# A graph layer's loop with slot 5's sums moved among the products with x, and an end with the left-over sums between the second layers

## The chip, the cores and the metric

One core of a Trainium2 chip runs the kernel. The metric is the device time of one execution in microseconds (us); below it stands as the median of three timed runs. The profile is of one more execution, whose own time is given beside its span.

## The reference

The kernel computes one layer of a graph network over 12,500 nodes and 412,500 edges, which come sorted by their target node `dst`. All numbers are float32, and all edges read the same graph's globals.

```python
h = jnp.maximum(_layernorm(x, axis=-1), 0.0)                    # x: 12500 x 128
agg = jax.ops.segment_sum(edges, dst, num_segments=12500)       # edges: 412500 x 48
u = graph_globals[0]                                            # the same 64 numbers for every node
hid = jax.nn.relu(jnp.concatenate([h, agg, u], axis=1) @ W1 + b1)   # 256 wide
out = x + hid @ W2 + b2                                         # 12500 x 128
```

## The kernel before

**Tiles.** A chunk is 768 edges, 128 partitions of 6; a group is 4 chunks. One iteration of the loop takes 11 groups (33,792 edges) and 1,024 nodes; there are 12 iterations. The very first group is summed ahead of the loop (`prologue`); the last 3,924 edges (5 chunks and 84 more) and 212 nodes are done in the end (`epilogue`). The 11 groups lie in six slots, each with its own buffer: slots 0 to 3 and slot 5 hold two groups, slot 4 one. The nodes of an iteration are block A and block B of 512; the 212 left over are block Z.

**The sum over edges, in two steps.** `sums(s)` multiplies, for each chunk and each of its six edges a partition, a one-hot matrix of 28 columns with 128 x 48 edge numbers (line 681); four chunks lie beside each other in the columns of the array. This gives partial sums in PSUM bank `S[s % 2]`, which ScalarE copies to `ss[s]` (line 685). `place(s)` multiplies these by a one-hot window `pl[s]` of 186 columns (line 703) and so adds them into the banks `agg[0]` (`ax`, block A) and `agg[1]` (`ay`, block B). VectorE makes both kinds of one-hot matrix, `onehots(s)` (line 662) and `places(s)` (line 668); both look one iteration ahead, except that slot 5's last groups reach over into the next iteration's nodes: `place(5, .., 1)` puts their part for this iteration at its end, `place(5, (0,), 0)` the other part at the start of the next.

**The layers.** `stats`, `variance`, `shift` (VectorE, with a square root on ScalarE) and `norm` (ScalarE, line 731) make the normalized x; `turn` transposes it on TensorE (line 740) and copies it back (line 741); `sums_out` copies the aggregates from PSUM (`ags`, line 746). `layers(layer_x)` is four products of W1 with x (line 750), into the banks PH0, PH1, PT, PO; `layers(layer_e)` adds W1 times the aggregates (line 755); `layers(relu)` is ScalarE's bias and relu (line 760). `second` is the product with W2 (line 776), and it runs one iteration later: near the start of an iteration for the nodes of the one before. Its result is added to x + b2 (`add_b`, GpSimd, line 735) and held in SBUF (`hold`, line 780). All held blocks are stored in the end, by `store_held`.

**What sets the order.** The order in which `body` calls these functions is the order of instructions on every engine: each engine takes its own part of the list in turn and waits at the first instruction whose semaphores are not there. `Flow` works out these waits from the names that each operation reads and writes. Loads of edges go out on SP in the order of `add_slots`; a slot's next load waits until its sums are done. Loads of x go out on ScalarE's queue. TensorE's loop is cut at `f.mark = "su4"`, the sums of slot 4: its instructions from there on are the first part of the code that it jumps back to.

In `body`, TensorE's order is sums 0, 1, 2; place 5 (first part), 0, 1; second layers A, B; sums 3, 4, 5; turns A, B; place 2, 3, 4, 5 (second part); products with x; products with the aggregates. In `epilogue` it is the left-over sums (`sur`, line 938), place 5, the turn of Z, the left-over places (`pcr`, line 948), both layers' first products of Z, second layer A, a transpose for the verdict on the indices (`verdict_2`), second layer B, second layer Z.

Of the kernel before, what the change touches and what calls it, by code (L numbers as in the profile page):

```python
# [18 lines left out]
P = 128  # L19
# [7 lines left out]
IN = 1024  # L27
# [25 lines left out]
class Flow:  # L53
# [14 lines left out]
    def op(self, eng, name, reads, writes, emit, dma=False):  # L68
        self.seq.append(dict(eng=eng, name=name, r=tuple(reads), w=tuple(writes), emit=emit, dma=dma, it=self.at))
# [336 lines left out]
def kernel(  # L406
# [40 lines left out]
    S = [bank("s0"), bank("s1")]  # L447
    agg = [bank("ax"), bank("ay")]
    pt = bank("pt")
    ph = [bank("ph0"), bank("ph1")]  # L450
# [60 lines left out]
    A, B, Z = 0, 1, 2  # L511
# [113 lines left out]
    def verdict_1():  # L625
        farthest()
        f.chain("DVE", "wc", ["worst", "farm"], ["wcol"],
            lambda: nc.vector.tensor_scalar(wcol, farm, -(V - 1) / 2, None, OP.add),
            lambda: nc.vector.tensor_tensor(wcol, wcol, worst[:, 2:3], OP.max))
# [40 lines left out]
    def onehots(s):  # L670
        g = SLOTS[s]
        onehot(s, oh[s], ["rel_i"], rel_i[:, g[0] - 1:g[0]] if len(g) == 1 else rel_i[:, g[0] - 1:g[1]:g[1] - g[0]])

    def places(s):
        windows(s, pl[s], ["off_i"], [off_i[:, v - 1:v] for v in SLOTS[s]])
# [15 lines left out]
    def place(s, fresh=(), part=None):  # L691

        groups, sv, pv = SLOTS[s], ss[s], pl[s]
        todo = [(n, j) + v for j, g in enumerate(groups) for n, v in enumerate(pieces(g)) if part is None or v[0] == part]
        todo.sort(key=lambda v: v[2] if len(groups) == 1 else (v[0] if v[1] == 0 else 1 - v[0], v[1]))
        seen = set()

        def emit(i):
            seen.clear()
            out = []  # L700
            for _, j, bk, at, frm, w in todo:
                h = HI * bk
                out.append(nc.tensor.matmul(agg[bk][h:h + DE, at:at + w], sv[:, j], pv[:, j, frm:frm + w],  # L703
                                            start=bk in fresh and bk not in seen, stop=True, skip_group_check=True))
                seen.add(bk)
            return out
        op("PE", f"pc{s}" + ("" if part is None else f".{part}"), [f"ss{s}", f"pl{s}"], [f"bk{b}" for b in sorted({v[2] for v in todo})], emit)
# [21 lines left out]
    def norm(k, m=P):  # L729
        op("ACT", f"xn{k}", [f"x{k}", f"x{k}t", f"sc{k}", f"sh{k}"], [f"xn{k}"], lambda i: [  # L730
            nc.scalar.activation(xn[k][:m, r], xt[k][:m, r], AF.Relu, bias=sh[k][:m, r:r + 1], scale=sc[k][:m, r:r + 1]) for r in range(RR[k])])  # L731
# [5 lines left out]
    def turn(k, m=P, bk=None, key="PT", eng="ACT"):  # L737
        pv = (pt if bk is None else bk)[:, :RR[k] * P].rearrange("p (r c) -> p r c", r=RR[k])
        copy = nc.scalar.copy if eng == "ACT" else nc.vector.tensor_copy
        op("PE", f"tu{k}", [f"xn{k}", "ident"], [key], lambda i: [nc.tensor.transpose(pv[:, r, :m], xn[k][:m, r], ident[:m, :m]) for r in range(RR[k])])  # L740
        op(eng, f"hT{k}", [key], [f"hT{k}"], lambda i: [copy(hT[k][:, :, :m], pv[:, :, :m])])

    def sums_out(k, m=P):
        h, r = HI * (k % 2), RR[k]
        op("ACT", f"ag{k}", [f"bk{k % 2}"], [f"ag{k}"], lambda i: [
            nc.scalar.copy(ag[k // 2][h:h + DE, :, :m], agg[k % 2][h:h + DE, :m * r].rearrange("p (c r) -> p r c", r=r))])
# [17 lines left out]

    middle = [(a, k) + v for a, bs in enumerate(((("PH0", ph[0]), ("PH1", ph[1])), (("PT", pt), ("PO", po)))) for k, v in enumerate(bs)]

    def layers(fn):

        for a, k, key, bk in middle:
            fn(f"{k}.{a}", key, bk.rearrange("p (r c) -> p r c", r=R), k, a)  # L770

    def second(k, m=P, bk=None, key="PO", keep=None):
# [15 lines left out]
    def prologue():  # L788
# [51 lines left out]
        for b in range(NB):  # L840
# [13 lines left out]
        windows(5, pl[5], ["off0"], [off[:, 0:1], off[:, 0:1]])  # L854
        op("PE", "bi", ["w1u", "u"], ["PH1"], lambda i: [
            nc.tensor.matmul(ph[1][:, NG + a:NG + a + 1], w1u[:, a * P:(a + 1) * P], u, start=True, stop=True, skip_group_check=True) for a in range(NH)])
        onehots(2)
        op("DVE", "bj", ["PH1", "b1"], ["bias"], lambda i: [nc.vector.tensor_tensor(bias, ph[1][:, NG:NG + NH], b1_sb, OP.add)])
        dst_3(ph[1], "PH1", range(1, NB))
        fetch_off(1)  # L860
        places(0)
        places(1)
        op("DVE", "spare", [], ["spare"] + [f"di{b}" for b in range(NB)] + [f"di{NB - 1}r", f"di{NB - 1}s"] + [f"df{k}" for k in range(DF)],
           lambda i: [nc.vector.memset(hold[0][:, 0:1], 0.0)])
        for s in (3, 4, 5):
            onehots(s)
        for s in (2, 3, 4):
            places(s)
        op("DVE", "f0", ["rel0.0", "rel0.3"], ["farm"], lambda i: [nc.vector.tensor_reduce(farm, rel[:, :q], AX.X, OP.max, apply_absolute_value=True)])

    def body(it):
        f.at = it

        def add_slots(*some):
            for s in some:
                sums(s)
                if it < NIT - 1:
                    load_e(s, 1)

        keep = lambda i: (i + NIT - 2) % (NIT - 1)  # L880
        farthest()
        fetch(1)
        add_slots(0, 1)
        for k in (A, B):
            stats(k)
            variance(k)
        add_slots(2)
        onehots(0)
        shift(A)
        shift(B)  # L890
        onehots(1)
        onehots(2)
        norm(A)
        norm(B)
        place(5, (0,), 0)
        place(0, (1,))
        place(1)
        places(5)
        fetch_off(1)
        places(0)  # L900
        places(1)
        for k in (A, B):
            second(k, P, ph[k], f"PH{k}", keep)
        for k in (A, B):
            add_b(k)

        add_slots(3, 4, 5)
        for s in (3, 4, 5):
            onehots(s)
        turn(A)  # L910
        turn(B, P, po, "PO")
        if it < NIT - 1:
            load_x(A, lambda i: (i + 1) % NIT * IN)
            load_x(B, lambda i: (i + 1) % NIT * IN + BN)
        for s in (2, 3, 4):
            place(s)
        place(5, (), 1)
        sums_out(A)
        sums_out(B)
        for s in (2, 3, 4):  # L920
            places(s)
        layers(layer_x)
        layers(layer_e)
        layers(relu)

    def epilogue():
        f.at = NIT
        m = RN // RZ
        load_rest()
        store_held()  # L930
        add_b(Z, m)
        stats(Z, m)
        variance(Z, m)
        shift(Z, m)
        norm(Z, m)
        rest = lambda j, c: P if j * CG + c < FULL else TP
        op("PE", "sur", ["oh0", "oh1", "e0.0", "e0.1", "ezt"], ["S0"], lambda i: [
            nc.tensor.matmul(S[0][NV * c:NV * c + V, j * DE:(j + 1) * DE], oh[j][:rest(j, c), c * T + t], e[0][:rest(j, c), j * CG + c, t * DE:(t + 1) * DE],  # L938
                             start=(t == 0), stop=(t == T - 1), skip_group_check=True)
            for j in range(2) for t in range(T) for c in range(min(CG, RC - j * CG))])  # L940
        op("ACT", "ssr", ["S0"], ["ssr"], lambda i: [nc.scalar.copy(ssr.rearrange("p j d -> p (j d)"), S[0][:, :2 * DE])])
        place(5, (0,), 0)
        turn(Z, m, S[1], "S1")
        verdict_0()
        verdict_1()
        todo = [(j,) + v for j, g in enumerate((1, 2)) for v in pieces(g)]
        op("PE", "pcr", ["ssr", "pl0", "pl1"], ["bk0"], lambda i: [
            nc.tensor.matmul(agg[bk][:DE, at:at + w], ssr[:, j], pl[j][:, 0, frm:frm + w], start=False, stop=True, skip_group_check=True)
            for j, bk, at, frm, w in todo])
        sums_out(Z, m)  # L950
        zr = [S[0][:, a * RN:(a + 1) * RN].rearrange("p (r c) -> p r c", r=RZ) for a in range(NH)]
        for a in range(NH):
            layer_x(f"z{a}", "S0", zr[a], Z, a, a == 0, m)
        for a in range(NH):
            layer_e(f"z{a}", "S0", zr[a], Z, a, m)
        for a in range(NH):
            relu(f"z{a}", "S0", zr[a], Z, a, m)
        second(A, P, ph[A], "PH0")
        store(A, lambda i: (i - 1) * IN)
        verdict_2()  # L960
        second(B, P, ph[B], "PH1")
        store(B, lambda i: (i - 1) * IN + BN, eng="ACT")
        second(Z, m, pt, "PT")
        store(Z, lambda i: i * IN, m)
        for e_ in f.of:
            op(e_, f"rb{e_}", ["bad"], [], lambda i, e_=e_: [f.of[e_].reg_load(flag_of[f.of[e_].engine], bad[0:1, 0:1])])
# [48 lines left out]
```

## Time and profile before

| | |
|---|---|
| timed runs | 277.99, 278.39, 282.0 us; median 278.39 |
| profiled execution | 277.39 us, its span 275.6 us |
| TensorE busy | 252.7 us, 92% of the span |
| VectorE busy | 239.5 us, 87% |
| ScalarE, GpSimd busy | 128.2 us, 47%; 54.5 us, 20% |
| DMA | 94.33 MB, 342 GB/s over the span |

The span runs from the first to the last instruction; the profiled execution's time is 1.8 us longer. Rows of a timeline give the start, the length, the engine, the line of the kernel, the operation, the tiles as out<-in, the shape, the number of instructions merged into the row, and in brackets the engine's idle time before it with what ended it. A table by stretches gives for each stretch its length, then busy time and instructions of TensorE's products, its weight loads, VectorE, ScalarE and GpSimd, then the granted TensorE clock, the DMA engines' busy share and GB/s. The lengths of TensorE's rows overlap, since products are pipelined; the distance from start to start is what a step takes.

### The profile page before, as it was taken

The numbers are of one execution on the slowest core, as the hardware profiler recorded it, in microseconds if no ns is written. First come the engines' busy times: TensorE is split into PE (matmuls) and PEld (weight loads), VectorE is DVE, ScalarE is ACT, GpSimd is POOL, SyncE is SP. The second block draws the span as 40 slices with busy tenths as digits, with TensorE's granted clock in tenths as the row PEclk, the third lists the DMA queues.
The fourth block names the chain that finished last, engine by engine and source line by source line (L and its number), as shares of the span: only waits on it lengthen the run. The fifth ranks groups of instructions, "written<-read, shape, count | busy, mean of one in ns | idle before, by whom it ended". The sixth has DMA issues, their size and how long they took to land.

```text
span 275.6 us, 17205 instructions
## 1 busy us (share of the span) xinstructions
PE 252.7 (92%) x7567; PEld 195.6 (71%) x7568; DVE 239.5 (87%) x591; ACT 128.2 (47%) x316; POOL 54.5 (20%) x47
## 2 busy tenths in 40 slices
PE   2946999999999999999999999999999999999990
PEld 2946866867858849859768768578498497597580
DVE  4899997998989989989989979989899899799521
ACT  7800544535437337245445355373373463454520
POOL 8100050040220400500500502304105005007000
PEclk9955999999999999999999999999999999999999
DMA  6999999999999999999999999999999999995992
GB/s 213 297 363 356 341 357 362 356 357 361 356 361 357 356 362 356 356 362 356 356 362 356 356 362 356 359 359 356 362 357 356 362 356 356 362 356 208 368 363 73
DMA packets 79012, 94.33 MB, mean 342 GB/s; under 512 B 3227, under 2 KB 72189, under 8 KB 78998
## 3 DMA queue, kind: packets, MB, share of 16 engines
q1 hardware_dynamic: 75398, 87.63, 96.1%
q10 hardware_dynamic: 3312, 6.03, 6.2%
q0 software_dynamic: 288, 0.49, 0.7%
q8 instruction: 7, 0.11, 0.2%
q14 instruction: 7, 0.06, 0.1%
HBM read 87.75 MB, written 6.40 MB: 342 GB/s over the span
## 4 chain that ended last, share of the span: by engine, by line
PE 87%; SPq 5%; DMA 3%; issue 2%; DVE 0%
PE s L681 27%; PE ph L776 18%; PE ph L750 8%; PE ax L703 7%; SPq L516 5%; PE ph L755 5%; PE po L750 4%; PE pt L750 4%; PE pt L755 4%; DMA e<-in_edge_attr_dram 3%; PE ay L703 3%; PE pt L740 3%; PE po L740 2%; PE s L938 1%; PE s L750 0%
## 5 line engine op out<-in xcount | busy, mean ns | idle before, releaser
L662 DVE TENSOR_TENSOR oh<-iota_v,rel_i 128x1344 f32<-128x1344 f32 (+1 forms) x78 | 130.8, 1716 | 0.0
L681 PEld LDWEIGHTS s<-e,oh 128*28 128x28 f32 x6336 | 75.1, 109 | 23.3 <-issue 21.4
L681 PE MATMUL s<-e,oh 128*28 128x48 f32 x6336 | 80.9, 210 | 11.0 <-issue 6.7
L735 POOL TENSOR_TENSOR xba<-xa,b_sb 128x512 f32<-128x512 f32 x12 | 15.4, 1285 | 198.3 <-DVE holda L780 198.3
L685 ACT COPY ss<-s 128x96 f32<-128x96 f32 (+1 forms) x72 | 16.8, 234 | 70.6 <-PE s L681 70.6
L668 DVE TENSOR_SCALAR pl<-iota_w,off_i 128x186 f32<-128x186 f32 x141 | 35.1, 309 | 0.5
L735 POOL TENSOR_TENSOR xbb<-xb,b_sb 128x512 f32<-128x512 f32 x12 | 31.1, 2591 | 0.0
L760 ACT ACTIVATE hida<-ph,bias 128x512 f32<-128x512 f32 x12 | 8.2, 687 | 42.2 <-PE ph L755 42.2
L703 PE MATMUL ax<-pl,ss 128*48 128x186 f32 (+3 forms) x172 | 27.1, 300 | 0.0
L776 PEld LDWEIGHTS ph<-w,hida 128*128 128x128 f32 x208 | 24.2, 191 | 3.8 <-issue 3.8
L776 PE MATMUL ph<-w,hida 128*128 128x128 f32 x208 | 26.7, 281 | 0.0
L703 PE MATMUL ay<-pl,ss 128*48 128x186 f32 (+3 forms) x168 | 26.3, 297 | 0.0
L776 PE MATMUL ph<-w,hidb 128*128 128x128 f32 x208 | 25.6, 276 | 0.6 <-issue 0.6
L776 PEld LDWEIGHTS ph<-w,hidb 128*128 128x128 f32 x208 | 24.3, 192 | 0.8 <-issue 0.7
L731 ACT ACTIVATE xna<-xa,sha,sca 128x128 f32<-128x128 f32 x48 | 19.8, 482 | 5.1 <-DVE sha L727 5.1
L710 DVE BATCH_NORM_STATS2 sta<-xa 128x6 f32<-128x128 f32 x48 | 10.5, 281 | 12.1 <-DMA xa<-in_x_dram 12.1
L703 PEld LDWEIGHTS ax<-pl,ss 128*48 128x48 f32 x172 | 17.6, 126 | 4.3 <-issue 2.0
L731 ACT ACTIVATE xnb<-xb,shb,scb 128x128 f32<-128x128 f32 x48 | 19.6, 479 | 0.0
L703 PEld LDWEIGHTS ay<-pl,ss 128*48 128x48 f32 x168 | 17.8, 124 | 0.0
L755 PE MATMUL ph<-ags,w1a 48*128 48x512 f32 x48 | 13.5, 641 | 0.0
L750 PE MATMUL ph<-hta,w1h 128*128 128x512 f32 x24 | 13.5, 644 | 0.0
L750 PE MATMUL ph<-htb,w1h 128*128 128x512 f32 x24 | 12.3, 592 | 0.0
(150 smaller groups left out, 301.5 us busy)
## 6 DMA issues: line engine op xcount, KB each, us to landing
e<-in_edge_attr_dram SPq DMA_DIRECT2D x133, 576.0 KB, 10.0
xa<-in_x_dram ACTq DMA_DIRECT2D x11, 256.0 KB, 5.8
xb<-in_x_dram ACTq DMA_DIRECT2D x11, 256.0 KB, 6.3
out_dram<-holda SPq DMA_DIRECT2D x11, 256.0 KB, 3.2
out_dram<-holdb SPq DMA_DIRECT2D x11, 256.0 KB, 3.3
holda<-in_dst_dram SPq DMA_DIRECT2D x4, 384.0 KB, 4.9
e<-in_edge_attr_dram SPq DMA_DIRECT2D x1, 720.0 KB, 8.9
xa<-in_x_dram SPq DMA_DIRECT2D x1, 256.0 KB, 10.5
```

Of the source, the lines that this page charges most:

```text
L516: return [f.of[eng].dma_start(dst_ap(i) if callable(dst_ap) else dst_ap, src_ap(i) if callable(src_ap) else src_ap)]
L662: op("DVE", f"oh{name}", reads + ["iota_v"], [f"oh{name}"], lambda i: [nc.vector.tensor_tensor(ov, iota_v[:, None, None, :].to_broadcast([ ...
L668: nc.vector.tensor_scalar(out[:, j], iota_w, o[j], None, OP.is_equal) for j in range(len(o))])
L681: nc.tensor.matmul(S[k][NV * c:NV * c + V, j * DE:(j + 1) * DE], o[:, (j * CG + c) * T + t], ev[:, j * CG + c, t * DE:(t + 1) * DE], start ...
L685: op("ACT", f"ss{name}", [f"S{k}"], [f"ss{name}"], lambda i: [nc.scalar.copy(sv.rearrange("p j d -> p (j d)"), S[k][:, :m * DE])])
L703: out.append(nc.tensor.matmul(agg[bk][h:h + DE, at:at + w], sv[:, j], pv[:, j, frm:frm + w], start=bk in fresh and bk not in seen, stop=Tr ...
L731: nc.scalar.activation(xn[k][:m, r], xt[k][:m, r], AF.Relu, bias=sh[k][:m, r:r + 1], scale=sc[k][:m, r:r + 1]) for r in range(RR[k])])
L735: nc.gpsimd.tensor_tensor(xb[k][:m], xt[k][:m], b2_sb[:m, None, :].to_broadcast([m, RR[k], D]), OP.add)])
L740: op("PE", f"tu{k}", [f"xn{k}", "ident"], [key], lambda i: [nc.tensor.transpose(pv[:, r, :m], xn[k][:m, r], ident[:m, :m]) for r in range( ...
L750: nc.tensor.matmul(o, w1h[:, a * P:(a + 1) * P], hT[k][:, :, :m], start=first, stop=False, skip_group_check=True)])
L755: nc.tensor.matmul(o, w1a[h:h + DE, a * P:(a + 1) * P], ag[k // 2][h:h + DE, :, :m], start=False, stop=True, skip_group_check=True)])
L776: nc.tensor.matmul(ov[:m, r], hid[k][:, a, r, :m], w2[:, a], start=(a == 0), stop=(a == NH - 1)) for r in range(RR[k]) for a in range(NH)])
```

## The change

In the loop, slot 2's sums move from slot 1's side to behind the second layers; slot 1's place moves from slot 0's side to those of slots 2 to 4; slot 5's sums move behind the turns and these places, and the second part of slot 5's place moves in front of the last of the four products with x. The one-hot matrices follow: those of slot 2 go with slots 3 and 4, those of slot 5 and the windows of slot 1 go later. ScalarE copies block A's aggregates before slot 5's sums instead of after them. In the end, place 5 and the turn of Z come first, then second layer A, then the left-over sums, then second layer B, then the rest of Z's work. In the prologue the order of VectorE's one-hots follows the loop's.

TensorE's order in `body` after: sums 0, 1; place 5 (first part), 0; second layers A, B; sums 2, 3, 4; turns A, B; place 1, 2, 3, 4; sums 5; three products with x; place 5 (second part); the fourth product with x; products with the aggregates. No operation is added or left out.

```diff
-    def layers(fn):
+    def layers(fn, some=middle):
-        for a, k, key, bk in middle:
+        for a, k, key, bk in some:
...
     prologue:
-        onehots(2)
         op("DVE", "bj", ...)
         dst_3(ph[1], "PH1", range(1, NB))
         fetch_off(1)
         places(0)
-        places(1)
+        onehots(2)
         op("DVE", "spare", ...)
-        for s in (3, 4, 5):
+        for s in (3, 4):
             onehots(s)
-        for s in (2, 3, 4):
+        for s in (1, 2, 3, 4):
             places(s)
+        onehots(5)
...
     body:
-        add_slots(2)
         onehots(0)
         shift(A)
         shift(B)
         onehots(1)
-        onehots(2)
         norm(A)
         norm(B)
         place(5, (0,), 0)
         place(0, (1,))
-        place(1)
         places(5)
         fetch_off(1)
         places(0)
-        places(1)
         for k in (A, B):
             second(k, P, ph[k], f"PH{k}", keep)
         for k in (A, B):
             add_b(k)
 
-        add_slots(3, 4, 5)
-        for s in (3, 4, 5):
+        add_slots(2, 3, 4)
+        for s in (2, 3, 4):
             onehots(s)
         turn(A)
         turn(B, P, po, "PO")
         if it < NIT - 1:
             load_x(A, lambda i: (i + 1) % NIT * IN)
             load_x(B, lambda i: (i + 1) % NIT * IN + BN)
-        for s in (2, 3, 4):
+        for s in (1, 2, 3, 4):
             place(s)
+        sums_out(A)
+        for s in (1, 2, 3, 4):
+            places(s)
+        add_slots(5)
+        onehots(5)
+        layers(layer_x, middle[:3])
         place(5, (), 1)
-        sums_out(A)
         sums_out(B)
-        for s in (2, 3, 4):
-            places(s)
-        layers(layer_x)
+        layers(layer_x, middle[3:])
         layers(layer_e)
         layers(relu)
...
     epilogue:
         norm(Z, m)
+        place(5, (0,), 0)
+        turn(Z, m, S[1], "S1")
+        second(A, P, ph[A], "PH0")
+        store(A, lambda i: (i - 1) * IN)
...
         op("PE", "sur", ...)
         op("ACT", "ssr", ...)
-        place(5, (0,), 0)
-        turn(Z, m, S[1], "S1")
         verdict_0()
         verdict_1()
+        second(B, P, ph[B], "PH1")
...
         for a in range(NH):
             relu(f"z{a}", "S0", zr[a], Z, a, m)
-        second(A, P, ph[A], "PH0")
-        store(A, lambda i: (i - 1) * IN)
         verdict_2()
-        second(B, P, ph[B], "PH1")
         store(B, lambda i: (i - 1) * IN + BN, eng="ACT")
         second(Z, m, pt, "PT")
         store(Z, lambda i: i * IN, m)
```

## The prediction, made before the change was run

> **What bounds the kernel now.** I read the page, then the table by stretches of time (two iterations of the loop), the DMA issues, the waits, and last TensorE's timeline of one iteration and of the end.
>
> ```profile
> span 275.6 us, 17205 instructions
> PE 87%; SPq 5%; DMA 3%; issue 2%; DVE 0%
> ```
> ```profile
> 44.71:64.12 19.41, 19.00 (x617) 14.55 (x621) 18.04 (x45) 9.50 (x25) 3.84 (x2) 1.00 1.09 358
> 219.33:238.91 19.58, 19.09 (x619) 14.56 (x621) 18.00 (x44) 9.50 (x25) 3.84 (x2) 1.00 1.09 358
> ```
> ```profile
> e<-in_edge_attr_dram SPq DMA_DIRECT2D x133, 576.0 KB, 10.0
> xa<-in_x_dram ACTq DMA_DIRECT2D x11, 256.0 KB, 5.8
> xb<-in_x_dram ACTq DMA_DIRECT2D x11, 256.0 KB, 6.3
> ```
> ```profile
> PE s L681 <- DMA e<-in_edge_attr_dram: 4.2, 3, 2.5
> ```
>
> The chain that ended last is 87% TensorE. In a stretch of 19.41 us it is busy 19.00; VectorE 18.04, ScalarE 9.50; so a microsecond added to TensorE's stream lengthens an iteration. DMA is a close second bound: an iteration loads 11 x 576 KB of edges and 2 x 256 KB of x, 7.01 MB, which at the 358 GB/s of both rows takes 19.59 us. The early iteration, 19.41, is TensorE's own pace; the late one, 19.58, is the DMA's: edges loaded ahead have been used up. The waits agree: only three waits for edges are listed, 4.2 us, and none of them in the iteration shown next.
>
> One iteration on TensorE (start, length, what):
>
> ```profile
> 141.64 3.50 PE L681 MATMUL s<-e,oh 128*28 128x48 f32 x288
> 145.07 0.48 PE L703 MATMUL ax<-pl,ss 128*48 128x140 f32 x3
> 146.16 2.05 PE L776 MATMUL ph<-w,hida 128*128 128x128 f32 x16
> 148.04 1.95 PE L776 MATMUL ph<-w,hidb 128*128 128x128 f32 x16
> 149.92 1.22 PE L681 MATMUL s<-e,oh 128*28 128x48 f32 x96
> 151.55 1.74 PE L681 MATMUL s<-e,oh 128*28 128x48 f32 x144 [0.41 <-issue]
> 153.22 0.66 PE L740 MATMUL pt<-ident,xna 128*128 128x128 f32 x4
> 154.24 0.36 PE L703 MATMUL ax<-pl,ss 128*48 128x186 f32 x1
> 155.49 1.12 PE L750 MATMUL ph<-hta,w1h 128*128 128x512 f32 x2
> 156.45 1.02 PE L750 MATMUL ph<-htb,w1h 128*128 128x512 f32 x2
> 157.31 1.02 PE L750 MATMUL pt<-hta,w1h 128*128 128x512 f32 x2
> 158.17 1.02 PE L750 MATMUL po<-htb,w1h 128*128 128x512 f32 x2
> 159.12 1.13 PE L755 MATMUL ph<-ags,w1a 48*128 48x512 f32 x4
> ```
>
> From start to start: sums of slots 0 to 2 3.43, places 1.09, second layers 3.76, sums 3 with the loop's jump 1.63, sums 4 and 5 1.67, turns 1.02, places 1.25, products with x 3.63. In the last, a pair in mid-stretch takes 0.86 (156.45 to 157.31), but the first 0.96 and the last 0.95: entering a stretch costs 0.10, leaving it 0.09. The other stretches show the same. At 0.86/1024 = 0.84 ns a column the first places (3 times 2 x 186 columns, two banks at once where they can) are 0.94, and take 1.09; a second layer (16 x 128 columns) is 1.72, and the second one takes 1.88. **So each stretch of one kind costs about 0.15 us beyond its columns.**
>
> **The loop, part by part.** No matrix product is added or removed; the order changes. TensorE's stretches before: sums 0-2, places, second layers, sums 3, jump, sums 4-5, turns, places, x products, aggregate products. After: sums 0-1, places, second layers, sums 2-3, jump, sum 4, turns, places, *sum 5*, three x products, *places 5.1*, the *fourth x product*, aggregate products. Three stretches more, 3 x 0.15 = 0.45. Inside the sums one boundary between slots goes (1|2 and 4|5 are no longer neighbours, 2|3 become so); no row prices it alone: it saves between 0 and a whole stretch's 0.15, and as a slot takes 1.14 in slots 0-2 and 1.11 by 1.67/1.5 in 4-5, starts included, boundaries cannot be cheap; I take 0.15. Net +0.30: 19.70 us an iteration. Bounds: 0, if the new switches overlap, to +0.57, three at 0.19 without the saving.
>
> The Trainium skill speaks against the change here: TensorEngine Tiling, Key Properties, has it that a change of tiling mode drains TensorE. It gives no time; TensorE: Matmul & The Clock Gate, Single matmul latency, puts the part of a warm matmul outside its columns at 166 ns, and three of these, less 0.15, would be an estimate of +0.35, 0.6 us more over the loop than mine.
>
> A row of ScalarE's timeline, a relu over 128 x 512 out of PSUM (the last of the loop), bounds a copy of 48 x 512 from above:
>
> ```profile
> 259.34 0.70 ACT L760 ACTIVATE hidb<-po,bias 128x512 f32<-128x512 f32 x1
> ```
>
> The waits that move cost nothing as far as I see. Sum 2 stands at 3.43 x 2/3 + 0.78 (two of three places) + 3.76 = 6.9 us of the iteration instead of 2.3, sum 5 at 12.6 instead of 10.3: edges have 2 to 4 us more to land, and the DMA no longer sets the late iterations. SP issues loads in the same order, each behind its sum; a load waits 10.0 us from issue to landing, mostly in the queue, so an issue 1 or 2 us later leaves the queue full. VectorE's one-hots and places are used 9 us or more after they are written, most in the next iteration; without that cover each microsecond of them (18.04 busy) would be on the path. On ScalarE, places 5.1 need the copy of sum 5 and the aggregate products need the copy of places 5.1; three x products (2.6) cover the first, the fourth (0.86 + 0.19) the second, at most 0.70 for the copy plus a handover: 0.3 us to spare, and if not, that much an iteration. The x loads leave ScalarE earlier, since the adds of b2 follow second layers that come 1.5 us earlier; VectorE's wait for x shrinks, which no one waits for.
>
> The loop ends where the left-over sums start:
>
> ```profile
> 258.38 2.94 PE L938 MATMUL s<-e,oh 128*28 128x48 f32 x72
> ```
>
> From its second iteration (44.71) to there are 213.67 now, eleven at 19.70 = 216.7 after. **+3.0.**
>
> The first iteration, on arriving edges:
>
> ```profile
> 24.95 2.14 PE L681 MATMUL s<-e,oh 128*28 128x48 f32 x96 [0.40 <-DMA e<-in_edge_attr_dram]
> 33.50 1.22 PE L681 MATMUL s<-e,oh 128*28 128x48 f32 x96
> ```
>
> Sum 2 waits 0.40 for edges and takes 2.14 there, at about half the speed of a sum behind the second layers (33.50, 1.22). After, it stands behind them, with its edges there. Saved 2.1 + 0.4; paid: 1.1 for the sum there, 0.30 for the stretches, and some 0.3 because more of the layers runs at half speed. **-0.8**, between 0 and -1.5.
>
> **The end.** TensorE's rows behind the left-over sums, then ScalarE's and SP's:
>
> ```profile
> 261.25 0.53 PE L703 MATMUL ax<-pl,ss 128*48 128x140 f32 x4
> 261.70 0.40 PE L740 MATMUL s<-ident,xnr 106*128 106x106 f32 x2
> 262.03 0.83 PE L948 MATMUL ax<-pl,ssr 128*48 128x186 f32 x4
> 262.79 0.98 PE L750 MATMUL s<-htr,w1h 128*128 128x212 f32 x4
> 263.71 0.98 PE L755 MATMUL s<-agr,w1a 48*128 48x212 f32 x4
> 264.62 2.05 PE L776 MATMUL ph<-w,hida 128*128 128x128 f32 x16
> 266.62 1.95 PE L776 MATMUL ph<-w,hidb 128*128 128x128 f32 x16
> 268.40 1.04 PE L776 MATMUL pt<-w,hidr 128*106 128x128 f32 x8
> ```
> ```profile
> 260.65 0.88 ACT L731 ACTIVATE xnr<-xr,shr,scr 106x128 f32<-106x128 f32 x2 [0.43 <-DVE shr L727]
> 264.73 0.77 ACT L760 ACTIVATE hidr<-s,bias 128x212 f32<-128x212 f32 x2 [1.50 <-PE s L755]
> ```
> ```profile
> 269.93 0.77 SPq L516 DMA_DIRECT2D out_dram<-otr  x2
> ```
>
> Now TensorE never stands here: the left-over sums (2.87 to the next start) cover ScalarE, which must finish the loop's last relu (at 260.04) and then scale block Z's x until 261.53; both second layers cover the relu of Z (until 265.50). From the loop's end to the last store's issue are 269.93 - 258.38 = 11.55 us.
>
> After, the turn of Z stands second, in front of everything that covered its wait, and TensorE takes its queue in order: second layer A, sums, second layer B and all else stand behind it. From the loop's end: places 0.53, then nothing until x of Z is scaled at 3.15 (261.53 - 258.38), **2.6 us idle**; turn from 3.2 to 3.55; second layer A to 5.45 (1.89: 2.00 from 264.62 to 266.62, less a 0.11 transpose); sums to 8.3; second layer B to 10.2 (1.78 and a switch); places of the rest 0.76 and a switch to 11.1; x products to 12.0; aggregate products from 12.0, and the relu of Z ends 1.79 after their start (263.71 to 265.50), at 13.8, with nothing left to run but the verdict's transpose: **0.9 idle**; the last second layer from 13.85; the store issues 1.53 after that (268.40 to 269.93) and a switch: 15.45. **+3.9.** The adds and stores of A and B come earlier and end earlier; they are not last. The store of A stays behind the held ones on SP, and the store of B goes out on ScalarE behind the relu of Z at 13.9, before the last.
>
> **Sum:** 3.0 - 0.8 + 3.9 = 6.1. The profiled execution took 277.39, so 283.5; the three timed runs (277.99, 278.39, 282.0) stood 0.6 and more above it, so as a timed run **284.1 us**, 2.0% over the median. A measurement of this kernel tells about 2% from no change, so this sits on the line.
>
> **Rivals.**
> *The clock falls in the end's idle stretch.*
>
> ```profile
> 11.65:15.06 3.41, 2.76 (x63) 2.42 (x62) 3.38 (x4) 2.06 (x5) 0.00 (x0) 1.00 1.06 341
> 15.06:18.47 3.41, 1.57 (x80) 1.60 (x84) 3.34 (x12) 0.00 (x0) 0.00 (x0) 0.50 1.09 360
> 267.64:271.06 3.42, 1.80 (x17) 1.59 (x15) 1.24 (x3) 0.00 (x0) 0.00 (x0) 1.00 0.52 192
> 271.06:274.47 3.41, 0.00 (x0) 0.00 (x0) 0.00 (x0) 0.00 (x0) 0.00 (x0) 1.00 0.14 38
> ```
>
> The third number from the end is the granted clock. It fell at 15.06, after a stretch with 0.65 us idle, and did not at 271.06, after one with 1.6 idle. 2.6 idle may be enough; then 3.4 us run at half speed, +1.7: 285.8. The Trainium skill (TensorE: Matmul & The Clock Gate, The HAM clock gate) asks for at least one idle window of about 3.4 us; by that rule this does not happen. The row at 15.06 does not look like that rule, so I leave it 0.2.
>
> *Not slower: the switches in the loop hide under weight loads, and only the waits count.* The place is the loop; it decides if an added stretch costs under 0.03 us. Eleven iterations at TensorE's 19.40 are 213.4 and no longer stretched to the DMA's 19.58 at the end, as edges now have 2 us more: -0.3 - 0.8 + 3.9 = 2.8, 281.0 by the same steps, +0.9%. For it: weight loads do run under products. Against: the 0.96 and 0.95 beside 0.86. 0.25.
>
> *The loads starve.* SP stands in front of load 2 until sum 2 is done at 8.05 of the iteration; if that empties the queue for 0.3 us an iteration, +3.3: 287.4. Against: 10.0 us in the queue. 0.05.
>
> *The end does not stall,* ScalarE having been freed earlier: then 284.1 - 2.6 = 281.5. The order of ScalarE's queue is not changed there: 0.05.
>
> **How the numbers follow.** My forecast 0.45. Range 280.3 to 287.4: from the case of hidden switches, with the first iteration's whole 1.5, to starved loads or the clock on top of switches at their dear bound. Over 2% slower (above 283.96): 0.6 of my 0.45, nearly all of the clock's 0.2 and of the starved loads' 0.05, and a little of the rest: 0.53. Within 2%: 0.45, faster 0.02, as the end costs 3.9 whatever the loop does.
>
> **What would show it.** Iterations start 19.70 apart to the last, not 19.41 growing to 19.58, and DMA falls to 356 GB/s; VectorE's wait for x is gone; TensorE is idle 2.6 us ahead of the turn of Z, ended by ScalarE's scaling, and 0.9 ahead of Z's second layer, ended by its relu; the last store issues 15.4 after the loop's end. I am wrong if iterations stay at 19.4 (the switches), if they pass 19.9 (a wait that I don't see, at places 5.1 first), or if the turn of Z follows its places at once.

## The result and the profile after

| | before | after |
|---|---|---|
| timed runs, median | 278.19 us | 286.57 us (286.04 to 289.14) |
| ratio | | 1.0326, 95% interval 1.0248 to 1.0405: slower |
| span of the profiled execution | 275.6 us | 284.2 us |
| start of the second iteration | 44.64 | 44.56 |
| loop from there to its end | 213.74 | 218.79 |
| loop's end to the last store's issue | 11.55 | 15.32 |

Before has a fourth run here, of 277.63 us, and so a median of 278.19. The forecast was 284.1, with +6.1 us over before's profiled execution; the span grew by 8.5. The page of after, its head and its chain of work that ended last:

```profile
span 284.2 us, 17193 instructions
PE 83%; DVE 6%; issue 3%; DMA 3%; ACT 3%; SPq 0%; DVEq 0%; ACTq 0%
```

The chain still runs through TensorE. VectorE's 6% are one-hot matrices and statistics of the first iteration; ScalarE's 3% are mostly the first iteration's scaling and the two waits in the end. The table by stretches, one iteration of after, then the whole loop of after and of before:

```profile
44.56:64.42 19.86, 19.46 (x614) 14.49 (x612) 19.38 (x53) 9.51 (x25) 3.84 (x2) 1.00 1.09 358
44.56:263.35 218.79, 214.46 (x6735) 159.35 (x6733) 194.26 (x475) 104.65 (x265) 44.76 (x23) 1.00 1.07 355
44.64:258.38 213.74, 209.15 (x6735) 160.09 (x6733) 197.64 (x474) 104.51 (x265) 43.52 (x23) 1.00 1.07 354
```

The same 6,735 matrix products take 5.31 us more of TensorE's busy time, and the loop gets 5.05 longer: TensorE is not waiting more, it is occupied longer by the same work. One iteration of after on TensorE, by the timeline:

```profile
183.76 2.40 PE L681 MATMUL s<-e,oh 128*28 128x48 f32 x192
186.09 0.48 PE L703 MATMUL ax<-pl,ss 128*48 128x140 f32 x3
186.87 2.05 PE L776 MATMUL ph<-w,hida 128*128 128x128 f32 x16
190.64 2.36 PE L681 MATMUL s<-e,oh 128*28 128x48 f32 x192
193.39 0.71 PE L681 MATMUL s<-e,oh 128*28 128x48 f32 x48 [0.39 <-issue]
194.04 0.66 PE L740 MATMUL pt<-ident,xna 128*128 128x128 f32 x4
195.06 0.36 PE L703 MATMUL ax<-pl,ss 128*48 128x186 f32 x1
196.30 1.22 PE L681 MATMUL s<-e,oh 128*28 128x48 f32 x96
197.46 1.12 PE L750 MATMUL ph<-hta,w1h 128*128 128x512 f32 x2
200.23 0.52 PE L703 MATMUL ay<-pl,ss 128*48 128x140 f32 x4
200.69 1.12 PE L750 MATMUL po<-htb,w1h 128*128 128x512 f32 x2
201.74 1.13 PE L755 MATMUL ph<-ags,w1a 48*128 48x512 f32 x4
203.66 1.55 PE L681 MATMUL s<-e,oh 128*28 128x48 f32 x111
```

From start to start this gives 19.90 us. By kind, against the iteration of before shown in the prediction (19.40):

| | before | after | more |
|---|---|---|---|
| sums (after: 2.33 + 2.75 with the jump + 0.65 + 1.16) | 6.73 | 6.89 | 0.16 |
| places (0.78 + 1.24 + 0.46) | 2.34 | 2.48 | 0.14 |
| products with x (2.77 + 1.05) | 3.63 | 3.82 | 0.19 |
| second layers, turns, aggregate products | 6.70 | 6.71 | 0.01 |

Each of the three kinds that got one stretch more pays for one: 0.14 to 0.19. The one wait, 0.39 at the jump, is as before (0.41). The list of waits of after, TensorE's and then VectorE's:

```profile
PE s L681 <- DMA e<-in_edge_attr_dram: 1.3, 1, 1.3
DVE oh L662 <- PE s L681: 11.8, 20, 0.8
DVE sta L710 <- DMA xa<-in_x_dram: 4.7, 9, 0.6
```

Edges are waited for once, ahead of the loop's second iteration; loads are on time ever after. VectorE has a new wait, its one-hots for the sums that free their buffers, 11.8 us in 20 times, and waits less for x (4.7, before 12.1). Neither reaches TensorE.

The end of after, on TensorE, then SP's last store:

```profile
263.35 0.52 PE L703 MATMUL ax<-pl,ss 128*48 128x140 f32 x4
266.56 0.40 PE L740 MATMUL s<-ident,xnr 106*128 106x106 f32 x2 [2.68 <-ACT xnr L731]
266.79 1.97 PE L776 MATMUL ph<-w,hida 128*128 128x128 f32 x16
268.69 2.94 PE L941 MATMUL s<-e,oh 128*28 128x48 f32 x72
277.06 1.12 PE L776 MATMUL pt<-w,hidr 128*106 128x128 f32 x8 [0.66 <-ACT hidr L760]
```
```profile
278.67 0.74 SPq L516 DMA_DIRECT2D out_dram<-otr  x2
```

Both waits stand where the prediction put them: 2.68 us ahead of the turn of Z, ended by ScalarE's scaling, and 0.66 ahead of Z's second layer, ended by its relu.

### The profile page after: what moved, and what is told of

Read it like the earlier page. It is cut to its first block, busy times and chain, and to the rows that moved or that the text cites. A ratio compares the mean times of both kernels' runs of the same rounds, so it can differ in the third digit from the quotient of the medians.

```text
span 284.2 us, 17193 instructions
## 1 busy us (share of the span) xinstructions
PE 259.7 (91%) x7567; PEld 195.3 (69%) x7568; DVE 236.1 (83%) x591; ACT 128.2 (45%) x316; POOL 55.9 (20%) x47
## 4 chain that ended last, share of the span: by engine, by line
PE 83%; DVE 6%; issue 3%; DMA 3%; ACT 3%; SPq 0%; DVEq 0%; ACTq 0%
PE s L681 26%; PE ph L776 16%; PE ph L750 8%; PE ax L703 7%; PE ph L755 4%; PE po L750 4%; PE pt L750 4%; PE pt L755 3%; DMA holda<-in_dst_dram 3%; PE ay L703 3%; DVE oh L662 3%; PE pt L740 2%; PE po L740 2%; PE s L941 1%; DVE pl L668 1%
## 5 line engine op out<-in xcount | busy, mean ns | idle before, releaser
L662 DVE TENSOR_TENSOR oh<-iota_v,rel_i 128x1344 f32<-128x1344 f32 (+1 forms) x78 | 124.8, 1627 | 11.8 <-PE s L681 11.8
L681 PE MATMUL s<-e,oh 128*28 128x48 f32 x6336 | 82.7, 209 | 8.4 <-issue 6.6
L735 POOL TENSOR_TENSOR xbb<-xb,b_sb 128x512 f32<-128x512 f32 x12 | 31.7, 2639 | 0.0
L703 PE MATMUL ay<-pl,ss 128*48 128x186 f32 (+3 forms) x168 | 28.5, 298 | 0.0
L776 PEld LDWEIGHTS ph<-w,hida 128*128 128x128 f32 x208 | 25.8, 202 | 3.6 <-issue 3.6
L776 PE MATMUL ph<-w,hida 128*128 128x128 f32 x208 | 28.2, 292 | 0.0
L746 ACT COPY ags<-ay 48x512 f32<-48x512 f32 x12 | 7.0, 581 | 34.9 <-PE ay L703 34.9
```

Source lines behind the costliest of these rows:

```text
L662: op("DVE", f"oh{name}", reads + ["iota_v"], [f"oh{name}"], lambda i: [nc.vector.tensor_tensor(ov, iota_v[:, None, None, :].to_broadcast([ ...
L681: nc.tensor.matmul(S[k][NV * c:NV * c + V, j * DE:(j + 1) * DE], o[:, (j * CG + c) * T + t], ev[:, j * CG + c, t * DE:(t + 1) * DE], start ...
L735: nc.gpsimd.tensor_tensor(xb[k][:m], xt[k][:m], b2_sb[:m, None, :].to_broadcast([m, RR[k], D]), OP.add)])
L776: nc.tensor.matmul(ov[:m, r], hid[k][:, a, r, :m], w2[:, a], start=(a == 0), stop=(a == NH - 1)) for r in range(RR[k]) for a in range(NH)])
```

## The experiments

**1 and 2: the halves of the change.** First the loop (and prologue) of after with the end of before, then the other way round.

```diff
 # loop only: body and prologue as in after; epilogue as in before
 # end only: body and prologue as in before; epilogue as in after:
         norm(Z, m)
+        place(5, (0,), 0)
+        turn(Z, m, S[1], "S1")
+        second(A, P, ph[A], "PH0")
+        store(A, lambda i: (i - 1) * IN)
         op("PE", "sur", ...)
...
+        second(B, P, ph[B], "PH1")
```

> The changed loop with the end of before. If loop and end cost independently (theory: three added stretches on TensorE in the loop, a stall in the end): iterations 19.89 us apart as in the changed kernel, 11.5 us from the loop's end to the last store's issue as before, so 286.6 - 3.8 = 282.8 us, ratio 1.016. Rival, the late end comes from the loop's order (something the loop leaves behind, say on ScalarE): the end stays near 15 us and the time near 286.

> The loop of before with the changed end. Theory: iterations 19.40 growing to 19.58, the end 15.3 instead of 11.5 with 2.7 us idle ahead of the turn of Z and 0.7 ahead of Z's second layer: 278.2 + 3.8 = 282.0 us, ratio 1.014. Rival, the held stores set the end and not TensorE: under 1 us more than before, 279.

Loop only: 282.3 us, ratio 1.0116 (1.0039 to 1.0192); iterations start 19.86 to 19.90 apart, the end takes 11.55 as before. End only: 283.22, ratio 1.0163 (1.0085 to 1.0241); iterations 19.39 to 19.46 apart. So the loop's part is in the order of the loop and the end's part in the order of the end. But the end alone took 16.81 and not 15.3:

```profile
261.91 0.40 PE L740 MATMUL s<-ident,xnr 106*128 106x106 f32 x2 [2.68 <-ACT xnr L731]
262.15 2.73 PE L776 MATMUL ph<-w,hida 128*128 128x128 f32 x16
264.81 3.67 PE L942 MATMUL s<-e,oh 128*28 128x48 f32 x72
```
```profile
259.75:263.17 3.42, 1.26 (x11) 1.26 (x12) 0.33 (x2) 2.02 (x6) 0.00 (x0) 1.00 1.02 383
263.17:266.58 3.41, 3.41 (x63) 2.87 (x61) 1.59 (x6) 0.00 (x0) 0.00 (x0) 0.50 1.01 377
```

The same wait of 2.68, and behind it the granted clock (third number from the end) is 0.50 for 3.41 us: second layer A takes 2.73 instead of 1.97 and the left-over sums 3.67 instead of 2.94, 1.49 together. This is the prediction's first rival; after, with the same code in its end, escaped it in its profiled execution.

**3: two stretches more, nothing else.** The kernel before, with the second part of place 5 and the copy of block B's aggregates between the third and fourth product with x.

```diff
-        place(5, (), 1)
         sums_out(A)
-        sums_out(B)
...
-        layers(layer_x)
+        layers(layer_x, middle[:3])
+        place(5, (), 1)
+        sums_out(B)
+        layers(layer_x, middle[3:])
```

> Before, with one step of the change alone: the second part of place 5 (and the copy of block B's aggregates behind it) stands between the third and the fourth product with x. Sum 5 stays with sums 3 and 4. Theory of the stretches: two stretches more, 0.14 + 0.20 us an iteration, 19.74 instead of 19.40, from the first iteration on: 12 x 0.34 less the 0.3 us of DMA waits that go, 278.2 + 3.8 = 282.0, ratio 1.013. Rival, the switches overlap with weight loads and the changed loop loses its time in waits around sum 5 that now stands alone: within 0.5 us of before, 278.7.

281.81 us, ratio 1.0102 (1.0067 to 1.0136). Iterations start 19.72 apart from the first to the last: 0.32 over 19.40 for two stretches.

```profile
199.46 1.02 PE L750 MATMUL pt<-hta,w1h 128*128 128x512 f32 x2
200.41 0.53 PE L703 MATMUL ay<-pl,ss 128*48 128x140 f32 x4
200.87 1.12 PE L750 MATMUL po<-htb,w1h 128*128 128x512 f32 x2
201.92 1.13 PE L755 MATMUL ph<-ags,w1a 48*128 48x512 f32 x4
```

TensorE goes from the third product to the place, to the fourth and on to the aggregates without any idle time: no wait for ScalarE's copies. The third product now ends a stretch and takes 0.95 instead of 0.86; the fourth is a stretch of its own and takes 1.05 instead of 0.95.

**4: the turn of Z behind the left-over sums.** After, with the turn of Z moved behind what covered ScalarE's scaling.

```diff
         place(5, (0,), 0)
-        turn(Z, m, S[1], "S1")
         second(A, P, ph[A], "PH0")
         store(A, lambda i: (i - 1) * IN)
         op("PE", "sur", ...)
         op("ACT", "ssr", ...)
+        turn(Z, m, S[1], "S1")
```

> The changed kernel with one line of its end moved: the turn of Z stands behind the left-over sums instead of ahead of second layer A. Theory: the 2.7 us in which TensorE waits for ScalarE's scaling of Z go, the 0.7 us ahead of Z's second layer stay: 286.6 - 2.7 = 283.9 us, ratio 1.021. Rival, the wait only moves (to the first product with Z's x, behind the copy of the turn): 0.5 us gained at most, 286.

283.81 us, ratio 1.0182 (1.0107 to 1.0257); the end takes 13.25, 2.07 less than after's. The missing 0.6 has a name:

```profile
264.20 2.05 PE L776 MATMUL ph<-w,hida 128*128 128x128 f32 x16 [0.61 <-ACT hida L760]
274.70 1.12 PE L776 MATMUL pt<-w,hidr 128*106 128x128 f32 x8 [0.66 <-ACT hidr L760]
```

Second layer A now comes half a microsecond after the loop's last products, and the loop's own relu of block A is not done yet. In after the wait for Z stood over this wait and hid it.

**5: sum 5 alone.** After, with slot 5's sums and one-hots beside slot 4's again.

```diff
-        add_slots(2, 3, 4)
-        for s in (2, 3, 4):
+        add_slots(2, 3, 4, 5)
+        for s in (2, 3, 4, 5):
             onehots(s)
...
-        add_slots(5)
-        onehots(5)
         layers(layer_x, middle[:3])
```

> The changed kernel with the sums of slot 5 back beside those of slot 4 (and their copy and one-hots); place 5's second part stays among the products with x. Theory of the stretches: one stretch less than the changed loop, 19.90 - 0.15 = 19.75 us an iteration, near the 19.72 of the kernel that moved place 5 alone; end 15.3 as in the changed kernel: 286.6 - 1.8 = 284.8 us. Rival, a wait of place 5 or of the aggregates' copy behind sum 5 makes the loop slow: with sum 5 early no wait is left and the loop falls by 0.4 or more, under 282.

285.72 us, ratio to the kernel before 1.0296 (1.0281 to 1.0311). Iterations are 19.72 to 19.74 apart but for one of 19.81, 0.16 to 0.18 less than after's:

```profile
182.36 2.38 PE L681 MATMUL s<-e,oh 128*28 128x48 f32 x192
202.10 1.10 PE L681 MATMUL s<-e,oh 128*28 128x48 f32 x84
```

The timed runs scatter too much to price a stretch: 1.8 us less than after's median was expected, and the median is 0.85 less.

This kernel and experiment 3's have the same two stretches more than before and as many boundaries between slots inside their stretches; here slot 2's sums stand beside slot 3's, there beside slot 1's, and both take 19.72. What the change takes away is the boundary between slots 4 and 5, which this kernel has and after has not. Were it worth a stretch's 0.15, as the prediction took it, giving it up for one more stretch would cost nothing; it costs 0.16 to 0.18. The single products in the traces show what a boundary is worth. Inside a slot, the next product starts at most 0.03 us after the one before it. From slot 0 to slot 1 of before it takes 0.12 to 0.13 in most iterations, from slot 1 to slot 2 0.11 in all but the last two, and from slot 2 to slot 3 of after 0.12; but from slot 4 to slot 5 of before no step is longer than those inside a slot.

**6: one stretch fewer.** The kernel before, with the turns directly behind the second layers; both kinds are products of 128 rows with 128 columns.

```diff
             second(k, P, ph[k], f"PH{k}", keep)
+        turn(A)
+        turn(B, P, po, "PO")
...
-        turn(A)
-        turn(B, P, po, "PO")
```

> Before, with the turns of A and B moved directly behind the second layers (both use the whole array), so that one stretch of TensorE is saved. Theory: iterations of 19.25 instead of 19.40 until the loads bind at 19.58; behind the last edges' landing the turns' 1.0 us is gone: loop's end 1.1 us earlier, 277.3 us, ratio 0.996. Rival, a turn is a kind of its own and costs its stretch wherever it stands: iterations stay at 19.40, and the gain is under 0.5 us.

277.57 us, ratio 0.9995 (0.997 to 1.002): no difference. Yet the first nine of the eleven iterations behind its first are 0.2 to 0.27 shorter. The table by stretches has one of them, and TensorE's timeline what stands in the tenth:

```profile
103.72:122.86 19.14, 18.84 (x614) 14.51 (x612) 17.78 (x45) 9.52 (x25) 3.83 (x2) 1.00 1.09 358
221.38 1.23 PE L681 MATMUL s<-e,oh 128*28 128x48 f32 x96 [0.34 <-DMA e<-in_edge_attr_dram]
```

Of the 0.26, 0.11 is the wait at the jump (0.30 instead of 0.41); 0.15 is the stretch. Then TensorE has used up the edges loaded ahead and waits for DMA, and the last two iterations are 19.58 and 19.57, next to the DMA's 19.59 of the prediction. This execution's loop ended at 257.82, before's at 258.38; its second iteration had begun at 46.28 against 44.64.

**7 and 8: two products with x ahead of the loop's jump.** Turns among the second layers, then the two products into PT and PO; in the second kernel the load of the last 84 edges also does not wait for the left-over load ahead of it.

```diff
-        for k in (A, B):
-            second(k, P, ph[k], f"PH{k}", keep)
+        second(A, P, ph[A], "PH0", keep)
+        turn(A)
+        second(B, P, ph[B], "PH1", keep)
+        turn(B, P, po, "PO")
+        layers(layer_x, middle[2:])
...
-        layers(layer_x)
+        layers(layer_x, middle[:2])
 # second kernel also:
-        dma("SP", "lezt", [], ["e0.1", "ezt"], ...)
+        dma("SP", "lezt", [], ["ezt"], ...)
```

> Before, with the aim of the change by fewer stretches instead of more: the turns stand among the second layers, and the two products with x that need PT and PO directly behind them, all of them on the whole array; the other two products with x stay behind the places to cover the aggregates' copies. Sums 5 so stand 2.7 us later in the iteration than before. Theory: seven stretches, 19.25 us an iteration until the loads bind; loop's end about 2 us earlier than before, 276.3 us, ratio 0.992. Rival, TensorE waits for block B's copy of the turn or for the relus' banks: iterations of 19.6 and more, 279 or over.

> The same as the kernel with early products with x, and in the end the load of the last 84 edges no longer waits on SP for the left-over load ahead of it to land, so that the stores of the held blocks go out some 8 us earlier. Theory: the held stores land by 261 to 267 instead of 269 and the end is TensorE's alone: 275.5 us, ratio 0.989. Rival, the held stores then share the queue with nothing that matters, and the time is that of the kernel without it, 276.3.

291.35 us, 1.0491 (1.0464 to 1.0518), and 291.52, 1.0466 (1.0433 to 1.0499). Both expectations failed. The waits of the first:

```profile
PE pt L740 <- ACT xna L731: 12.1, 11, 1.8
DVE sta L710 <- DMA xa<-in_x_dram: 23.2, 11, 2.7
```

In each of 11 iterations TensorE waits for block A's scaled x, because the x of the next iteration lands too late for a turn this early. The turns of before have less slack than I took them to have; experiment 6, where they moved up only past the sums, has no such wait.

**9, 10 and 11: the left-over sums, and what ends behind them.** In the left-over sums' second half, a chunk of 128 rows and the last one of 14 rows alternate, two of the trace's products of one and two of the other. Experiment 9 is before with these ordered chunk by chunk; 10 adds the turns of experiment 6; 11 adds the load of the last 84 edges without its wait, which lets the held blocks' stores go out earlier.

```diff
-            for j in range(2) for t in range(T) for c in range(min(CG, RC - j * CG))])
+            for j in range(2) for c0 in range(0, min(CG, RC - j * CG), CG if j == 0 else 1) for t in range(T)
+            for c in range(c0, c0 + (CG if j == 0 else 1))])
```

> The kernel before, with the left-over sums of the second group ordered chunk by chunk, so that products of 128 rows and of 14 rows no longer alternate. Theory (a change of kind costs TensorE time, at whatever size of product): the 24 products of that half, which take 2.16 us in pairs of about 0.13 and 0.06, fall to about 1.0 to 1.3 us; the end gets shorter by about 0.9, the median about 277.1, ratio 0.9965. Rival (the pairs are slow because two quarters of the array wait for each other, or because of the 14 rows themselves): the sum of this half stays at 2.0 or more, ratio 1.000.

> The kernel before, with the turns of the loop directly behind the second layers (one stretch fewer) and the left-over sums ordered as in the run above. Theory: iterations 19.14 until the edges loaded ahead are used up, then 19.58 (DMA), and 0.9 less in the end: about 276.6, ratio 0.996. Rival (what the loop saves comes back in full as a wait for DMA, and the order of the left-over sums does nothing): 277.6, ratio 1.000.

> As the run above, and the load of the last 84 edges no longer waits for the load ahead of it to land, so that the stores of the held blocks are issued earlier. Theory (with the loop shorter, what ends last is partly the DMA's work, and its idle 2 us near 252 are given back): about 276.1, ratio 0.994. Rival (the stores are off the path, TensorE's end decides): the same time as the run above within 0.1 us.

277.81 us, ratio 1.0001 (0.9977 to 1.0024); 277.36, 0.9981 (0.9955 to 1.0007); 277.44, 0.9987 (0.9964 to 1.001). The expected 277.1, 276.6 and 276.1 were not reached. TensorE's end in experiment 10:

```profile
258.08 1.82 PE L938 MATMUL s<-e,oh 128*28 128x48 f32 x72
261.29 0.40 PE L740 MATMUL s<-ident,xnr 106*128 106x106 f32 x2 [0.93 <-ACT xnr L731]
```

The order shortens the sums as expected: 1.82 instead of 2.94, with the products of 14 rows as quick as those of 128, so the 14 rows themselves were not what was slow. And 0.93 of the 1.12 comes back at once: the sums had covered ScalarE's scaling of block Z, the same cover that the change took away whole. The end takes 11.43 instead of 11.55. In experiment 11 SP's first store is issued at 245.02 instead of 251.62 and the time does not move: the stores were not what ended last.

In the profiled execution of experiment 9, which took 281.84 us against the kernel's median of 277.81, the clock fell behind this wait, with only 0.93 idle in the stretch ahead of the fall, and stood at half until 270.88:

```profile
260.64:264.06 3.41, 2.49 (x28) 1.75 (x25) 1.69 (x10) 2.19 (x8) 0.00 (x0) 1.00 1.02 381
```

**12: cover for both of Z's waits.** Experiment 10, with second layer A in front of the turn of Z and second layer B left behind Z's aggregate products.

```diff
         place(5, (0,), 0)
+        second(A, P, ph[A], "PH0")
         turn(Z, m, S[1], "S1")
...
-        second(A, P, ph[A], "PH0")
         store(A, lambda i: (i - 1) * IN)
         verdict_2()
         second(B, P, ph[B], "PH1")
```

> The kernel with turns behind the second layers and the left-over sums by chunk, in which TensorE then stood 0.93 us in front of the turn of Z; here second layer A stands in front of that turn, second layer B stays behind Z's aggregate products. Theory (a stretch of 1.9 us that is ready covers ScalarE's scaling, and one second layer of 1.8 us covers Z's relu, which ends 1.79 us after the aggregate products' start): the wait of 0.93 is gone, one stretch more costs 0.15; loop's end to last store 11.43 to about 10.65; median about 276.6, ratio to the kernel before 0.995. Rival (the wait comes back in front of Z's second layer, or the stores of the held blocks end last): 11.4 again, 277.4, ratio 0.998.

276.4 us, ratio 0.9944 (0.993 to 0.9958): under 2%, but clear of its interval, and the lowest ratio of all kernels here.

```profile
257.98 1.82 PE L938 MATMUL s<-e,oh 128*28 128x48 f32 x72
260.19 2.05 PE L776 MATMUL ph<-w,hida 128*128 128x128 f32 x16
262.08 0.35 PE L740 MATMUL s<-ident,xnr 106*128 106x106 f32 x2
268.36 0.77 SPq L516 DMA_DIRECT2D out_dram<-otr  x2
```

TensorE has no wait left between the loop's end and the last store's issue, 10.38 us. Second layer A, which the change also pulled forward, is good cover when it follows the left-over sums (the loop's relu is done by then) and precedes the turn of Z; in the change it followed the turn. What bounds this kernel next is DMA: the largest share of its chain of work that ended last is now SP's queue of loads, and TensorE waits for edges late in the loop as in experiment 6 (0.35 us at 221.56).

```profile
SPq 47%; PE 38%; DMA 8%; issue 5%; DVE 0%
```

## Why the prediction was right, and where its terms were off

*A stretch of one kind costs about 0.15 beyond its columns: shown.* Two added cost 0.32 (experiment 3), sum 5's alone 0.16 to 0.18 (experiment 5; some 0.03 of it is a longer step that is told below), one removed gave 0.15 (experiment 6, by its rows). The Trainium skill's rule that a change of tiling mode drains TensorE (TensorEngine Tiling, Key Properties) fits these numbers.

*"Net +0.30: 19.70 us an iteration", loop +3.0: the term that failed.* It was +0.46 at first and +0.50 from the third iteration on, and the loop +5.05. What failed is the 0.15 that the prediction took back for a boundary between slots. Boundaries inside a stretch do cost something, as it argued, about 0.1 us from slot 0 to 1, 1 to 2 and 2 to 3 by the single products; but the one from 2 to 3 took the place of the one from 1 to 2, and the one that went, from 4 to 5, had cost nothing. Why it is free, no run shows. I had inferred one price for all from 1.14 and 1.11 us a slot, which also contain the entry and exit of their stretch, spread over three and one and a half slots. Of the 2.05 us that the loop was mis-sized by, 11 x 0.15 = 1.65 is this. Most of the rest is one step: from the third iteration on, the step from slot 0 to slot 1 takes 0.16 in after instead of 0.12, 0.36 us in nine iterations. Its cause stays open. Without it the three stretches cost 0.46, 0.15 each, as forecast. (The prediction counts before's loop from 44.71; its first product starts at 44.64, so its 213.67 is 0.07 short.)

*First iteration -0.8: it was -0.08.* TensorE's rows of after:

```profile
25.96 3.67 PE L776 MATMUL ph<-w,hida 128*128 128x128 f32 x16
29.47 1.95 PE L776 MATMUL ph<-w,hidb 128*128 128x128 f32 x16
```

The second layers did start 3.0 us earlier (25.96, before 28.91). But their first ran at half clock almost whole, as the clock rose at 29.385, in before at 28.712: from start to start it took 3.51 and not 1.89. The other one gave half of this back, as before's second layer B stands 0.56 us idle in this iteration; together the layers cost 0.8 where I had 0.3. Sums, places and products behind them took 2.07 more where I had 1.4, partly for place 1, which I had left out: 0.48 saved at its old position, 0.31 paid at its new one. This term moves from one execution to the next: the second iteration began at 44.62, 44.56 and 44.26 in three kernels with after's loop, at 44.64, 45.12 and 45.89 in three with before's (before itself, experiments 2 and 9). One profile each cannot price this term to better than that; -0.08 is inside the bounds of 0 to -1.5.

*The end +3.9: right, +3.77, by the steps given.* 2.68 idle (2.6 foreseen) and 0.66 (0.9 foreseen); experiment 4 showed that the first is the lost cover, and also that the relu of the loop's block A was the next thing late, which I had not listed.

*The rivals.* That the switches hide is refuted by experiments 3, 5 and 6. Starving loads: none, one wait of 1.3 us in the first iteration; DMA's rate in a window stayed at 358 and did not fall to the 356 that I named as a sign. Iterations of 19.90 came up to the 19.9 that I named as a sign of a wait unseen; no list of waits shows one. An end without a stall: refuted by both rows. The falling clock did not happen in after's profiled execution and did in experiment 2's, at +1.5, which I had put at +1.7. Two sums around the rivals were wrong: hidden switches come to 280.8 by the steps given, not 281.0, which puts the low end of the range at 280.1; and the clock on top of dear switches comes to 285.8 + 11 x 0.27 = 288.8, above the 287.4 that the range ends at. Neither bears on the result.

So the forecast of 284.1 against 286.57 is off by the loop's 2.05 and the first iteration's 0.7, less 0.3 in the end and behind it; the sign and both mechanisms, stretches in the loop and lost cover in the end, were as written. Without the boundary term the same steps give 11 x 19.85 - 213.67 = 4.7 for the loop and 285.8 in all.

## What to carry to other kernels

Count an order of matrix products in stretches of one kind before counting its waits: each new stretch here cost about 0.15 us of the engine that sets the time, and three more an iteration lengthened the loop by 5.05 us, while the slack that the order bought for edges gave back only the 0.3 us that before's last two iterations are longer than the others, and the slack for x nothing. In a tail, write beside each long product what it covers on the other engines; shortening it or moving it past its dependant returns the gain as a wait (1.12 saved, 0.93 waited), and the fix is another ready stretch in the same place, not an earlier start. A saving in the loop is worth only what the next bound leaves: experiment 6 saved up to 0.26 an iteration until the loads set the pace.

## What the runs showed of the hardware that I had not expected

The granted clock changes only at whole multiples of 3.41 us from its other changes, in each of the 14 traces, and TensorE's busy time in the stretch ahead does not by itself tell when it falls. Six stretches, each from one such point to the next; the multiply-adds are an estimate from the shapes of the products in each:

| kernel | stretch | TensorE busy of 3.41 | multiply-adds, millions | clock next |
|---|---|---|---|---|
| after | 264.90 to 268.30 | 1.74 | 29.7 | 1.00 |
| end only | 259.75 to 263.17 | 1.26 | 19.9 | 0.50 |
| experiment 9 | 260.64 to 264.06 | 2.49 | 11.2 | 0.50 |
| after | 8.90 to 12.32 | 1.97 | 21.5 | 0.50 |
| experiment 8 | 272.22 to 275.64 | all | 10.1 | 0.50 |
| experiment 3 | 263.96 to 267.37 | all | 11.2 | 1.00 |

```profile
264.90:268.30 3.40, 1.74 (x16) 1.75 (x17) 0.33 (x2) 1.51 (x5) 0.00 (x0) 1.00 0.89 339
8.90:12.32 3.41, 1.97 (x14) 1.91 (x15) 2.72 (x10) 1.81 (x4) 0.00 (x0) 1.00 1.07 334
272.22:275.64 3.42, 3.42 (x52) 2.38 (x39) 1.70 (x10) 2.50 (x7) 0.00 (x0) 1.00 0.04 12
263.96:267.37 3.41, 3.41 (x31) 2.24 (x30) 1.70 (x10) 2.23 (x7) 0.00 (x0) 1.00 0.96 353
```

In after's first stretch most of the busy time is second layer A, 128 rows by 128 columns of the array in full use; in experiment 9's it is small products, many of 28 or 48 columns or rows. The first four rows would let one think that the work done decides and not the time busy. The last two speak against either as the whole rule: both stretches hold the same part of the end, from within the left-over sums to the left-over places, both are busy throughout, and the clock fell after one of them; and 11.2 million multiply-adds were followed by the full clock in experiment 3, 21.5 million by the half clock in after. What decides stays open; no run here was made to test it. The Trainium skill (TensorE: Matmul & The Clock Gate, The HAM clock gate) asks for at least one idle window of about 3.4 us before the clock falls; stretches of that length are what the trace shows, but experiment 9's fall came behind one that was busy for 2.49 of 3.41, and experiment 8's behind one that was busy throughout.

The price of alternating between kinds also shows at the smallest scale: 72 left-over products take 2.94 us when 12 of 14 rows alternate by twos with 12 of 128, and 1.82 in order by kind, which is 1.12 for ten changes of kind more, about 0.11 us each, against 0.15 for one more stretch in the loop. From one product to the next, the trace of before has 0.13 to 0.14 us at such a change.
